# A third of the du*B products of the third stage, moved from GpSimd to ScalarE and TensorE, in a four-block sequence kernel on Trainium2

## The chip, the cores and the metric

The kernel runs on one core of one Trainium2 chip. The metric is the device time of one execution in microseconds (us). Engines are named as in the profile: PE is TensorE (PEld its weight loads), DVE VectorE, ACT ScalarE, POOL GpSimd, and SP the engine whose queue issues most DMAs. Lines are those of the kernel before; in the changed kernel they stand one further down from L623 on.

## What is computed

The input is x of 2 x 1024 x 256. Four blocks follow each other, each adding its output to x after a layer norm: attention with 16 heads of 128 and a causal mask with a linear bias; a feed-forward block with ternary weights; a selective state-space block; and a feed-forward block that keeps two of four hidden values. The change is in the third. Cut to what matters, with 512 channels d (DI) and 16 states n (DN):

```
delta = softplus(dt_low @ dt_proj.T + bias)      # b, l, d
A = -exp(A_log)                                  # d, n
deltaA = exp(delta * A)                          # l, b, d, n
dBu = delta * Bm * x_conv                        # l, b, d, n;  Bm is b, l, n
h = deltaA * h + dBu                             # one step per token l
y = sum over n of h * C  + x_conv * D            # C is b, l, n
out = (y * silu(z)) @ out_proj.T
```

## The kernel before

**Chunks and stages.** The tokens are cut into four chunks of 512 (U), k = 0 to 3: first and second half of sequence 0, then of sequence 1. Attention of chunk k is built together with everything else of chunk k-1 (`rest(k-1)`: ternary feed-forward, state space, kept-two feed-forward). So there are five stages: attention of chunk 0 beside the weight quantization; three stages with attention(k) beside rest(k-1); and rest(3) alone. The **third stage** is attention(2) beside rest(1). There `short` is true: attention(2) is a first half, so its rows of scores are 128 to 512 wide. `tail_end` is true for rest(3) only.

**What orders the work.** Each generator yields a cost after every step (2.2 for a step of the state loop), and the build loop at the end of the kernel runs `rest` ahead until its share of `cost(k)` has reached the share of attention steps done. This fixes the order in which the program is written. A scheduler then sets the order of each engine's queue; on the chip each queue is served in that order. Buffers come from pools: a tile with `bufs` n waits until the tile n earlier of the same tag has been read. PSUM has eight banks of 128 x 512: tag "s" 2 (scores), "mm" 3 (transposes, projections, attention outputs), "y" 1, "r" 2 (everything of `rest`).

**The state loop** (`state_space`, L505 on) goes over 64 products, four groups c of 128 channels times 16 states n. Channels lie on partitions, tokens along the row. For product i the functions are:

- `ask_b`, `ask_c` (L668): SP fetches row n of B and of C from a DRAM copy `bcd`, broadcast to 128 partitions (bs and cs, 256 KB each). bs has 5 buffers and is asked for five products ahead.
- `enter` (L713): POOL multiplies db = du * bs. du = delta * x_conv is made in `steps(c)` (L550 to L554).
- `decay` (L727): ACT computes da = exp(a_neg * dl) into an "r" bank.
- `scan` (L732): DVE runs the recurrence hs = da * h + db along the row. Its start comes from the chunk before (carry).
- `weigh` (L746): POOL multiplies hc = hs * cs, with 5 buffers.
- `total` (L678): PE adds hc into the "y" bank, turned by four 128 x 128 transposes; after n = 15 `gate` copies the sum (L761), turns it back (L764, an "r" bank) and multiplies by sz (L768).

At step i the program has total(i-5), ask_b(i+5), enter(i+1), decay(i), scan(i-1), weigh(i-3), ask_c(i+1).

Before the loop PE computes dt (L534) and bcp (L627), the 32 rows of B and C; ACT copies them (bc, L632), SP writes them to `bcd` (L634), and the broadcasts read them from there.

**The last stage** (`tail_end`) makes no db on POOL. du is turned by PE (`turned`, dup L561) and copied by ACT (duT L565), so that tokens lie on partitions; B as columns (bT, L640, copied as bTs L645) is then one scalar per partition. For n % 5 == 2 ACT scales the four 128 x 128 blocks of duT by it (bu, L697) and PE turns them back into a bank (db, L701); for the others PE multiplies by a diagonal (db, L707). da then lies in SBUF.

Attention's part of a stage, per head: scores s (L357), mask and maximum on DVE (L361, L366), exponential on ACT (L370), transposes pt and copies pT (L288, L291), z (L299, copied as zs L304), projections pq, pk (L330), pv (L337), and o (L313), added to x by DVE (L319). For a first-half chunk kT and v are also stored for the next chunk (kd L345, vd L347, both on SP).

Of the kernel before, what the change touches and what calls it, by code (L numbers as in the profile page):

```python
# [26 lines left out]
DI, DN, DR, DC = 512, 16, 128, 4  # L27
# [14 lines left out]
def kernel(  # L42
# [32 lines left out]
    ps_s, ps_mm, ps_z = bank("s", 2), bank("mm", 3), bank("mm", 3)  # L75
    ps_y, ps_r = bank("y", 1), bank("r", 2)
# [26 lines left out]
    def fill_in():  # L103

        if held:
            with tc.issue_after(ended["by"].ins):
                held.pop(0)()
# [397 lines left out]
    def state_space(k):  # L505
        b, u = CH[k]
        first, last, tail_end = u == 0, u == NU - 1, k == len(CH) - 1
# [3 lines left out]
        with ExitStack() as mctx:  # L511
# [45 lines left out]
            def turned(c, du):  # L557

                tp = ps_r(f"dup_{k}_{c}")
                for t in range(UT):  # L560
                    nc.tensor.transpose(  # L561
                        tp[:, t * P : (t + 1) * P], du[:, t * P : (t + 1) * P], ident
                    )
                duT = row_of("duT", f"duT_{k}_{c}", 2)
                nc.scalar.copy(duT, tp)  # L565
                return duT


            with ExitStack() as ictx:
                mi = ictx.enter_context(tc.tile_pool(name="mi", bufs=1, side="right"))  # L570
                in_sb = mi.tile([P, KC, 2 * DI], F32, name=f"in_sb_{k}")
                nc.sync.dma_start(out=in_sb, in_=inT.rearrange("(c p) m -> p c m", p=P))
                xp_sb = mi.tile([P, NDC, NX], F32, name=f"xp_sb_{k}")
                nc.sync.dma_start(out=xp_sb, in_=xpT.rearrange("(c p) m -> p c m", p=P))
                nc.sync.dma_start(out=dt_sb, in_=dtT)
                nc.sync.dma_start(out=out_sb, in_=outT.rearrange("(c p) m -> p c m", p=P))
                xT, put = plain(mi, f"m{k}")
                layernorm_T(k, f"m{k}", put, ps_r)
                yield 3

                def in_proj(e):
                    pp = (spare(k) if e % 2 else ps_r)(f"in_{k}_{e}")
                    for c in range(KC):
                        nc.tensor.matmul(  # L584
                            pp, lhsT=in_sb[:, c, e * P : (e + 1) * P], rhs=xT[:, c, :],
                            start=(c == 0), stop=(c == KC - 1),
                        )
                    return pp

                for e in range(NDC):  # L590
                    xp = mi.tile([P, DC - 1 + U], F32, tag="xp", name=f"xp_{k}_{e}", bufs=2)
                    if first:
                        nc.gpsimd.memset(xp[:, : DC - 1], 0.0)
                    else:
                        nc.gpsimd.tensor_copy(xp[:, : DC - 1], tail[:, e, :])
                    nc.scalar.copy(xp[:, DC - 1 :], in_proj(e))
                    if not last:
                        nc.gpsimd.tensor_copy(tail[:, e, :], xp[:, U:])
                    acc = work(f"cv_{k}_{e}")
                    nc.vector.tensor_scalar(acc, xp[:, 0:U], cw(e, 0), None, ALU.mult)  # L600
                    for i in range(1, DC):
                        nc.vector.scalar_tensor_tensor(
                            acc, xp[:, i : i + U], cw(e, i), acc, op0=ALU.mult, op1=ALU.add
                        )
                    silus = [nc.scalar.activation(xs[:, e, :], acc, AF.Silu)]
                    yield 3
                for e in range(NDC):
                    silus.append(nc.scalar.activation(sz[:, e, :], in_proj(NDC + e), AF.Silu))
                    yield 2

                with tc.issue_after(silus[0].ins), tc.issue_after(silus[-1].ins):
                    marks.append(nc.scalar.preload_act_table_set("natural_log_exp_and_others"))
                dl_ps = ps_r(f"dtl_{k}")
                for c in range(NDC):
                    nc.tensor.matmul(
                        dl_ps, lhsT=xp_sb[:, c, :DR], rhs=xs[:, c, :],
                        start=(c == 0), stop=(c == NDC - 1),
                    )
                nc.any.tensor_copy(dtl, dl_ps)
                parts, turns = {0: steps(0)}, {}  # L620
                if tail_end:
                    fill_in()
                    turns[0] = turned(0, parts[0][1])  # L623
                yield 3
                bc_ps = ps_da(f"bcp_{k}")
                for c in range(NDC):
                    nc.tensor.matmul(  # L627
                        bc_ps[: 2 * DN, :], lhsT=xp_sb[:, c, DR:], rhs=xs[:, c, :],
                        start=(c == 0), stop=(c == NDC - 1),
                    )  # L630
                bc = mi.tile([2 * DN, U], F32, name=f"bc_{k}", padded_shape=[P, U])
                nc.any.tensor_copy(bc, bc_ps[: 2 * DN, :])  # L632

                nc.sync.dma_start(out=bcd.rearrange("a n t -> (a n) t"), in_=bc)  # L634
                if tail_end:

                    bT_ps = ps_da(f"bT_{k}")[:, : UT * DN].rearrange("p (t n) -> p t n", t=UT)
                    for t in range(UT):
                        for c in range(NDC):
                            nc.tensor.matmul(  # L640
                                bT_ps[:, t, :], lhsT=xs[:, c, t * P : (t + 1) * P],
                                rhs=xp_sb[:, c, DR : DR + DN], start=(c == 0), stop=(c == NDC - 1),
                            )
                    bT = mc.tile([P, UT, DN], F32, name=f"bTs_{k}")
                    nc.vector.tensor_copy(bT, bT_ps)  # L645
                yield 4
# [23 lines left out]
                    )  # L670
                return ask

            ask_b, ask_c = row(brow, 0, "bs", 5), row(crow, 1, "cs", 6 if tail_end else 4)

            def add(c, h, start, stop):

# [6 lines left out]

            by_tensor = lambda i: tail_end
            by_scalar = lambda n: n % 5 == 2

            def enter(i):
                c, n = prods[i]  # L690
                dl, du = parts[c]
                if tail_end and by_scalar(n):

                    db[i] = ps_mm(f"db_{k}_{c}_{n}")
                    bu = part("bu", f"bu_{k}_{c}_{n}", 2)
                    for t in range(UT):
                        nc.scalar.activation(  # L697
                            bu[:, t * P : (t + 1) * P], turns[c][:, t * P : (t + 1) * P], AF.Copy,
                            scale=bT[:, t, n : n + 1],
                        )  # L700
                        nc.tensor.transpose(  # L701
                            db[i][:, t * P : (t + 1) * P], bu[:, t * P : (t + 1) * P], ident
                        )
                elif by_tensor(i):
                    db[i] = ps_mm(f"db_{k}_{c}_{n}")
                    for t in range(UT):
                        nc.tensor.matmul(  # L707
                            db[i][:, t * P : (t + 1) * P], lhsT=turns[c][:, t * P : (t + 1) * P],
                            rhs=diag[:, n, t, :], start=True, stop=True,
                        )  # L710
                else:
                    db[i] = part("db", f"db_{k}_{c}_{n}", 4)
                    nc.gpsimd.tensor_tensor(db[i], du, brow.pop(i), ALU.mult)  # L713
# [9 lines left out]
            def decay(i):  # L723
                c, n = prods[i]
                name = f"da_{k}_{c}_{n}"
                da[i] = part("da", name, 4) if by_tensor(i) else ps_da(name)
                nc.scalar.activation(da[i], parts[c][0], AF.Exp, scale=a_neg[:, c, n : n + 1])  # L727

            def scan(i):
# [45 lines left out]
            for i in range(-5, len(prods) + DRAIN(k)):  # L775
                for lag, f in stages:
                    if 0 <= i - lag < len(prods):
                        f(i - lag)
                if i >= 0:
                    yield 2.2  # L780
                if 0 <= i < len(prods) and i // DN + 1 < NDC:
                    c = i // DN + 1
                    if i % DN == (DN // 4 if tail_end else DN // 2):
                        parts[c] = steps(c)
                        yield 3
                    if tail_end and i % DN == DN - 5:
                        turns[c] = turned(c, parts[c][1])
            for t in range(UT):
                op = (spare(k) if t % 2 else ps_r)(f"mo_{k}_{t}")
# [229 lines left out]
```

## Time and profile before

| | us |
|---|---|
| time, median of 3 runs | 1869.58 (1869.01 to 1869.77) |
| the profiled execution | 1872.9 |
| its span | 1870.9, TensorE clock 0.981 on the mean |
| L746 POOL hc, x256 | 363.9 busy, 1438 ns each |
| L713 POOL db, x192 (three stages) | 258.2 busy, 1352 ns each |
| L727 ACT da, x256 | 177.7 busy, 697 ns each |
| bs from bcd, x192, 256 KB each | 4.4 from issue to landing |
| cs from bcd, x256, 256 KB each | 3.8 from issue to landing |

The span runs from the first to the last recorded instruction; the profiled execution's own time is 2.0 us longer. Busy time is the sum of an engine's instructions in a stretch. The PE clock is the share of full speed that was granted. "Idle before" is the time in which an engine stood still ahead of a group of instructions, with the instruction or transfer that ended it.

### The profile page before, as it was taken

The page shows a single profiled execution, that of the slowest core. Times are in us where ns is not written, and L with a number is a line of the kernel's source. Part 1 is how long each engine was busy: PE and PEld are TensorE (multiplying, and loading weights), DVE is VectorE, ACT ScalarE, POOL GpSimd, SP SyncE. Part 2 cuts the span into 40 slices and gives each one's busy share as a digit, 9 for nine tenths or more (in the row PEclk, how much of TensorE's full clock was granted, in tenths as well). Part 3 has the DMA queues.
Part 4 walks back from the last instruction along what each step waited for, and adds up shares of the span by engine and source line. Part 5 has one row for each costly group of instructions (what it writes and reads, how often), then busy time and mean ns, then how long its engine had stood idle before and what let it go on. Part 6 is the DMA issues. An engine that isn't in the chain of part 4 may idle for free. (4 is left out here: it accounts for less than half of the span.)

```text
span 1870.9 us, 24286 instructions
## 1 busy us (share of the span) xinstructions
PE 1731.3 (93%) x7984; PEld 1156.0 (62%) x7984; DVE 1212.3 (65%) x2347; ACT 959.4 (51%) x1780; POOL 845.5 (45%) x685
## 2 busy tenths in 40 slices
PE   7999999999989999997878999999999999888999
PEld 4666666455656566755556566645665655566895
DVE  5766455677786473468886465567779546446975
ACT  3445474656563562554555446465556345335742
POOL 3324031578892000429996002247889200045970
PEclk9999999999999999999999999999999999888999
DMA  6443512466662311337876324246676320112541
GB/s 188 130 141 127 195 46 86 143 201 204 208 205 83 107 51 60 119 114 231 251 245 196 121 65 133 86 132 198 204 219 203 91 93 32 70 49 73 185 128 62
DMA packets 178285, 255.99 MB, mean 137 GB/s; under 512 B 16224, under 2 KB 90976, under 8 KB 177136
## 3 DMA queue, kind: packets, MB, share of 16 engines
q1 hardware_dynamic: 177008, 241.87, 41.3%
q0 software_dynamic: 1152, 12.58, 1.8%
q8 instruction: 63, 1.03, 0.2%
q14 instruction: 62, 0.51, 0.1%
HBM read 232.04 MB, written 22.35 MB: 136 GB/s over the span
## 5 line engine op out<-in xcount | busy, mean ns | idle before, releaser
L746 POOL TENSOR_TENSOR hc<-hs,cs 128x512 f32<-128x512 f32 x256 | 363.9, 1438 | 16.1 <-PE y L678 9.3
L357 PE MATMUL s<-kT,qT 128*128 128x512 f32 (+3 forms) x768 | 304.7, 498 | 17.1 <-DVE ss L361 15.3
L370 ACT ACTIVATE ss<-ss,nm 128x128 f32<-128x128 f32 (+7 forms) x256 | 198.4, 775 | 178.0 <-DVE nm L366 168.6
L713 POOL TENSOR_TENSOR db<-du,bs 128x512 f32<-128x512 f32 x192 | 258.2, 1352 | 51.8 <-DVE hs L732 43.0
L361 DVE SCALAR_TENSOR_TENSOR ss<-s,lower 128x512 f32<-128x512 f32 (+3 forms) x384 | 204.2, 548 | 112.1 <-PE s L357 110.7
L299 PE MATMUL z<-pT,v 128*128 128x512 f32 (+3 forms) x768 | 266.1, 494 | 10.9 <-ACT pT L291 10.1
L366 DVE CUSTOM_DVE_ANT_0 ss<-ss,alibi 128x128 f32<-128x128 f32 (+7 forms) x256 | 240.6, 942 | 3.4
L727 ACT ACTIVATE da<-dl,a_neg 128x512 f32<-128x512 f32 x256 | 177.7, 697 | 118.1 <-DVE hs L732 94.3
L299 PEld LDWEIGHTS z<-pT,v 128*128 128x128 f32 x768 | 143.4, 191 | 146.2 <-issue 94.1
L291 ACT COPY pT<-pt 128x512 f32<-128x512 f32 (+3 forms) x313 | 142.9, 476 | 174.0 <-PE pt L288 172.3
L288 PE MATMUL pt<-ident,ss 128*128 128x128 f32 x1152 | 181.0, 279 | 38.6 <-DVE x L319 22.9
L288 PEld LDWEIGHTS pt<-ident,ss 128*128 128x128 f32 x1152 | 140.5, 143 | 103.1 <-DVE x L319 38.0
L732 DVE TENSOR_TENSOR_SCAN hs<-da,db 128x512 f32<-128x512 f32 x128 | 154.0, 1211 | 56.6 <-POOL db L713 27.4
L357 PEld LDWEIGHTS s<-kT,qT 128*128 128x128 f32 x768 | 129.0, 195 | 81.0 <-issue 43.9
L732 DVE TENSOR_TENSOR_SCAN hs<-da,carry,db 128x512 f32<-128x512 f32 x128 | 159.0, 1268 | 25.2 <-POOL hc L746 14.4
L319 DVE SCALAR_TENSOR_TENSOR x<-o,rr,x 128x256 f32<-128x256 f32 x256 | 108.9, 475 | 80.7 <-PE o L313 80.6
L678 PE MATMUL y<-ident,hc 128*128 128x128 f32 x1024 | 144.3, 278 | 9.6 <-POOL hc L746 9.6
L337 PEld LDWEIGHTS pv<-wv,xT_a 128*128 128x128 f32 x1024 | 126.1, 194 | 41.4 <-issue 25.4
L448 POOL DMA_DIRECT2D guT<-guT_d x4 | 2.7, 674 | 302.2 <-DVE nm L366 111.0
L337 PE MATMUL pv<-wv,xT_a 128*128 128x128 f32 x1024 | 127.3, 277 | 9.9 <-DVE carry L741 6.5
L678 PEld LDWEIGHTS y<-ident,hc 128*128 128x128 f32 x1024 | 120.7, 145 | 15.3 <-POOL hc L746 12.8
L313 PE MATMUL o<-wo,zs 128*128 128x256 f32 x512 | 123.4, 381 | 4.5 <-ACT kT L333 3.3
(199 smaller groups left out, 2617.6 us busy)
## 6 DMA issues: line engine op xcount, KB each, us to landing
cs<-bcd SPq DMA_DIRECT2D x256, 256.0 KB, 3.8
bs<-bcd SPq DMA_DIRECT2D x192, 256.0 KB, 4.4
alibi<-alibi_d SPq DMA_DIRECT2D x32, 512.0 KB, 4.5
wq<-in_wqT_dram SPq DMA_DIRECT2D x64, 128.0 KB, 3.5
wk<-in_wkT_dram SPq DMA_DIRECT2D x64, 128.0 KB, 3.2
wv<-in_wvT_dram SPq DMA_DIRECT2D x64, 128.0 KB, 2.8
wo<-in_woT_dram SPq DMA_DIRECT2D x64, 128.0 KB, 2.8
alibi<-alibi_d SPq DMA_DIRECT2D x32, 256.0 KB, 3.6
```

The lines of the kernel that those rows point to most:

```text
L288: nc.tensor.transpose(tp[:, i, :], s[:, (kb0 + i) * P : (kb0 + i + 1) * P], ident)
L299: nc.tensor.matmul(zp[:, q0:], lhsT=st["v_all"][:, kb, :], rhs=st["pts"][kb // 4][:, kb % 4, q0:], start=(kb == 0), stop=(kb == last),)
L337: nc.tensor.matmul(vp[:, t, :], lhsT=xT[:, c, t * P : (t + 1) * P], rhs=st["v"][:, c, :], start=(c == 0), stop=(c == KC - 1),)
L357: nc.tensor.matmul(sp[:, :n], lhsT=st["qT"][:, j * P : (j + 1) * P], rhs=st["kT"][:, k0 : k0 + n], start=True, stop=True,)
L361: nc.vector.scalar_tensor_tensor(s[:, k0 : k0 + n], sp[:, :n], CLIP, lower[:, S - W + k0 : S - W + k0 + n], op0=ALU.min, op1=ALU.max,)
L366: pace["tile"] = nc.vector.tensor_tensor_reduce(out=s[:, :W], in0=s[:, :W], in1=st["alibi"][:, :W], scale=1.0, scalar=3.0e38, op0=ALU.add, ...
L370: nc.scalar.activation(s[:, :W], s[:, :W], AF.Exp, bias=nm, scale=-1.0, accum_out=st["rs"][:, j : j + 1])
L678: nc.tensor.matmul(yTs[c][:, t * P : (t + 1) * P], lhsT=h[:, t * P : (t + 1) * P], rhs=ident, is_transpose=True, start=start and t == 0, s ...
L713: nc.gpsimd.tensor_tensor(db[i], du, brow.pop(i), ALU.mult)
L727: nc.scalar.activation(da[i], parts[c][0], AF.Exp, scale=a_neg[:, c, n : n + 1])
L732: nc.vector.tensor_tensor_scan(out=hs[i], data0=da.pop(i), data1=db.pop(i), initial=0.0 if first else carry[:, n, c : c + 1], op0=ALU.mult ...
L746: nc.gpsimd.tensor_tensor(hc[i], hs.pop(i), crow.pop(i), ALU.mult)
```

## The change

For k = 1 (`short`) the products with n % 3 == 1, that is n = 1, 4, 7, 10 and 13 of each c, 20 of 64, are made as in the last stage's n % 5 == 2: du is turned and copied (duT, one buffer), ACT scales four blocks of it by B's columns (bu, one buffer), and PE turns them back, into an "r" bank. Their da goes to SBUF (two buffers); the other 44 da stay in "r" banks. No row of B is fetched for these 20, and bs has four buffers instead of five. bT is computed in this stage too, and `turned` is called right after `steps(0)`, ahead of bcp, and later at n = 11 for the next c. The last stage is as before.

```diff
-                duT = row_of("duT", f"duT_{k}_{c}", 2)
+                duT = row_of("duT", f"duT_{k}_{c}", 2 if tail_end else 1)
...
                 if tail_end:
                     fill_in()
+                if tail_end or short:
                     turns[0] = turned(0, parts[0][1])
...
                 nc.sync.dma_start(out=bcd.rearrange("a n t -> (a n) t"), in_=bc)
-                if tail_end:
+                if tail_end or short:
 
                     bT_ps = ps_da(f"bT_{k}")[:, : UT * DN].rearrange("p (t n) -> p t n", t=UT)
...
-            ask_b, ask_c = row(brow, 0, "bs", 5), row(crow, 1, "cs", 6 if tail_end else 4)
+            ask_b, ask_c = row(brow, 0, "bs", 4 if short else 5), row(crow, 1, "cs", 6 if tail_end else 4)
...
-            by_tensor = lambda i: tail_end
-            by_scalar = lambda n: n % 5 == 2
+            by_scalar = lambda n: (tail_end and n % 5 == 2) or (short and n % 3 == 1)
+            by_tensor = lambda i: tail_end or by_scalar(prods[i][1])
...
-                if tail_end and by_scalar(n):
-
-                    db[i] = ps_mm(f"db_{k}_{c}_{n}")
-                    bu = part("bu", f"bu_{k}_{c}_{n}", 2)
+                if by_scalar(n):
+
+                    db[i] = (ps_mm if tail_end else ps_r)(f"db_{k}_{c}_{n}")
+                    bu = part("bu", f"bu_{k}_{c}_{n}", 2 if tail_end else 1)
                     for t in range(UT):
                         nc.scalar.activation(
                             bu[:, t * P : (t + 1) * P], turns[c][:, t * P : (t + 1) * P], AF.Copy,
...
-                da[i] = part("da", name, 4) if by_tensor(i) else ps_da(name)
+                da[i] = part("da", name, 4 if tail_end else 2) if by_tensor(i) else ps_da(name)
...
-                    if tail_end and i % DN == DN - 5:
+                    if (tail_end or short) and i % DN == DN - 5:
                         turns[c] = turned(c, parts[c][1])
```

## The prediction

> **What bounds the kernel now.** I read the page's first part, then tables of windows until the stage of the change stood alone, then groups and waits inside it. The whole span:
>
> ```profile
> PE 1731.3 (93%) x7984; PEld 1156.0 (62%) x7984; DVE 1212.3 (65%) x2347; ACT 959.4 (51%) x1780; POOL 845.5 (45%) x685
> ```
>
> By the average TensorE bounds the kernel and GpSimd has room. The state loop of the third stage (834 to 1015 us) is another matter. Columns: window, length, busy PE, PEld, DVE, ACT, POOL (instructions), PE clock, DMA share, GB/s.
>
> ```profile
> 834.00:860.00 26.00, 22.21 (x114) 15.40 (x113) 20.49 (x28) 12.97 (x27) 23.52 (x19) 1.00 0.74 240
> 860.00:880.00 20.00, 14.24 (x69) 9.68 (x67) 17.70 (x24) 11.34 (x25) 19.92 (x16) 0.91 0.83 250
> ...
> 900.00:920.00 20.00, 16.08 (x81) 11.26 (x80) 15.93 (x22) 10.16 (x20) 19.79 (x16) 0.84 0.81 260
> ...
> 960.00:980.00 20.00, 12.61 (x60) 8.17 (x60) 17.00 (x22) 8.60 (x18) 19.80 (x16) 1.00 0.66 219
> 980.00:1000.00 20.00, 17.93 (x98) 12.66 (x98) 16.59 (x28) 13.38 (x27) 20.00 (x16) 1.00 0.81 245
> ...
> 1015.00:1030.00 15.00, 15.00 (x84) 12.12 (x83) 8.02 (x24) 5.74 (x15) 0.29 (x1) 1.00 0.28 90
> ```
>
> See POOL at 19.8 to 20.0 of 20 from 860 to 1000, PE at 12.6 to 17.9, and PE full as soon as POOL is done. Over 834:1015 the sums are POOL 174.5, DVE 147.4, PE 145.9, ACT 95.7 of 181 us: PE idles 35.1. The groups of that window (count | busy us, mean ns | idle before, releaser):
>
> ```profile
> L713 POOL TENSOR_TENSOR db<-du,bs 128x512 f32<-128x512 f32 x64 | 85.9, 1348 | 5.1 <-DMA bs<-bcd 4.6 <-POOL du L554 0.4
> L746 POOL TENSOR_TENSOR hc<-hs,cs 128x512 f32<-128x512 f32 x64 | 85.5, 1341 | 2.8 <-DMA cs<-bcd 2.8
> L732 DVE TENSOR_TENSOR_SCAN hs<-da,carry,db 128x512 f32<-128x512 f32 x64 | 80.4, 1271 | 17.8 <-POOL hc L746 14.4 <-POOL db L713 1.9 <-ACT da L727 1.4
> L727 ACT ACTIVATE da<-dl,a_neg 128x512 f32<-128x512 f32 x62 | 42.8, 691 | 34.5 <-DVE hs L732 34.4
> ```
>
> POOL does 128 multiplications back to back; the scans wait for its buffers. PE's largest waits, 820:1020 (total us, times, longest):
>
> ```profile
> PE y L678 <- POOL hc L746: 9.1, 8, 3.1
> PE pt L288 <- DVE x L319: 8.0, 6, 2.4
> ```
>
> Only the first is POOL's directly. Since PE is 94 to 98% busy in 1000:1200, ending the loop early pays only as far as PE loses idle time inside it.
>
> **The change, part by part.** For 20 of the 64 products (n = 1, 4, 7, 10, 13; four c) the POOL multiplication goes. What replaces it runs in the last stage already (1705:1812):
>
> ```profile
> L697 ACT ACTIVATE bu<-duT,bTs 128x128 f32<-128x128 f32 x48 | 15.7, 387 | 0.0
> L701 PE MATMUL db<-ident,bu 128*128 128x128 f32 x48 | 8.2, 284 | 1.0 <-DVE hs L732 1.0
> L561 PE MATMUL dup<-ident,du 128*128 128x128 f32 x12 | 1.8, 272 | 0.0
> ```
>
> *POOL*: 20 x 1.348 = 27.0 us go: 147.5 left.
> *ACT*: 80 x 0.327 (15.7/48) = 26.2, four duT copies at 0.58 = 2.3, 20 exponentials into SBUF at 0.718 instead of 0.691 = 0.5: 95.7 becomes 125 of 181. Hidden, as ACT has 85 idle; without that cover 29.
> *PE*: 80 transposes at 0.150 (36.3/242, the y transposes of this loop) to 0.171 (8.2/48) = 12.0 to 13.7; dup 16 x 0.15 = 2.4; bT 3.7 (once, as at 1701.2). Sum 18 to 20: 145.9 becomes 165.
> *Clock*: the granted mean is 0.94 here, and dips follow PE's idle moments (910:915 has 2.58 busy of 5, then 915:920 a clock of 0.50). Spread evenly over busy PE the missing 0.06 would be 145.9 x 0.06 = 9 us; as the dips lie at idle moments I count 0 to 7. So 158 to 165; I take 162.
> *DVE*: the bTs copy, 0.2; the scans cost the same from PSUM (1.266 in the last stage).
> *DMA*: 20 rows of 256 KB fewer. Four bs buffers for 44 rows span six products, five for 64 spanned five: the 4.6 us of waits for bs do not grow; bounds -4.6 and 0, I take 0.
>
> The Trainium skill ("TensorE: Matmul & The Clock Gate", Part 4: PE-mode transpose) speaks against this: about 275 ns for one transpose, and transposes do not keep the clock up. By it the 80 would cost 22 us and PE's sum be 9 higher. The rows record 272 to 293 ns each too, but overlapping: busy time per transpose is 0.15 to 0.17. And 1726:1746, with 175 matmuls of that size, half of them transposes, ran at clock 1.00.
>
> *The start, where something is moved.* In the changed queues PE turns du (dup) before it computes bcp, so bcp moves from right behind dt (825.2) to behind du. Three score rows on DVE are now ahead of sr, so du ends at about 833.5 (831.8 before); four transposes, 834.3; bcp 3.6, 837.9; bc 0.57, 838.5. Before, bc's end (829.4) to the first db (834.5) took 5.1: first db 843.6. On SP, two loads (an alibi row, wq) now stand ahead of the bcd write, and wk and the store of kd between it and the first bs; kd waits for kT, which waits for pk, which PE does behind bT: bT to 841.6, pk and kT to 843.2, then 3.3 from request to db as before: 846.5. The loop's start is 9 to 12 us late (best case 0, if SP's order costs nothing and bcp slips forward). PE does attention meanwhile (it was full in 820:834), so this is POOL's loss, not PE's: bank 27 - 9 to 12 = 15 to 18 for POOL's path.
>
> *New waits.* The loop's exponentials used two PSUM banks alternately, each waiting for the scan two back. Now a turned product holds one of the banks from its transposes to its scan, so 44 exponentials wait for the scan just ahead, and the next scan for them: up to 0.69 + handover. A handover is 0.04 (a scan ended at 882.31, the exponential began at 882.35); I bound it by 0.1 on each side, so 0 to 0.9 per exponential, 0 to 40 in sum. Queued on ACT behind them are score exponentials and pT copies that PE's z needs. The static order puts DVE's other work (147.4 - 80.4 = 67 us, 1.05 per product) mostly into those gaps, so I take them as covered. bu has one buffer, so ACT also waits for PE to turn the last one, and PE does z, pq, pk, pv and o in one piece of about 10 us per head; a scan behind it waits, but the order places DVE's x updates there.
>
> **Sum.** Next limits for the stage: POOL 147.5 + 9 to 12 late = 157 to 160; DVE 147; PE 162 at a share it can reach. It reached 0.92 in the fourth stage (202.2 of 220 in 1230:1450, POOL 0.83, DVE 0.77) and 0.90 in the last (90.2 of 100). 162/0.92 = 176 against 181: 5 us. Break-even: PE may idle 16 to 23 instead of 35. The profiled execution took 1872.9 (span 1870.9 and 2.0 around it), 3.3 over the median of 1869.58; I subtract the gain from either: 1867.9 by profile, **1864.6** by median.
>
> **Rivals.**
> *A (forecast, 0.42)*: PE becomes the bound at 0.90 to 0.94: 0 to 9 us, centre 5: 1864.6, own range 1861 to 1869. For: PE full after the loop, POOL no longer late. A difference under 0.2% (3.7 us), about what a measurement can tell, takes 0.08 of it.
> *B (0.16)*: PE packs to 0.95 at full clock, 158/0.95 = 166; POOL's path gives the same 15 us: 1855 (up to 1852). For: 1015:1030 and 1100:1200 run at 0.98 to 1.00. Against: DVE at 147/166 = 0.89 and in order.
> *C (0.12)*: the removed wait is replaced: PE waits for x, pT, zs (8.0, 3.7, 3.4 above y's 9.1) stay, share about 0.895: 181 again, 1870. This is also how it looks if the change relieves POOL and nothing else. 0.08 within, 0.02 to each side.
> *D, slower (0.30)*: the bank wait. Place: ACT's exponential behind DVE's scan. The stage is 9 late + DVE 147 + 44 x uncovered part; it decides from (181 - 156)/44 = 0.57 us each. At 0.8: 191, +10: 1880. Upper end with 12 and 0.9: 199, +18: 1887. For: ACT's 34.4 us of waits for scans show how tightly the two are coupled with two banks free.
>
> Faster 0.32 + 0.02 + 0.16 = 0.50; same 0.08 + 0.08 = 0.16; slower 0.02 + 0.02 + 0.30 = 0.34 (0.02 of A falls there). Range 1853 to 1885: it leaves out a quarter of B and a third of D, under 2 in 10.
>
> **What would show it.** Right: L713 in the stage x44, about 59 us; POOL near 0.84; PE 0.91 or more; clock about 1.00; first db 843 to 847; y's wait for hc below 5 us. D: scans waiting for exponentials 15 us or more (1.4 now). B: the last hc before 1002. Wrong altogether: PE busy over 170, or a first db later than 850.

## The result, and the profile after

The changed kernel takes 1877.17 us in the median of 7 runs (1874.44 to 1880.48), the kernel before 1870.37 in 7 runs. The ratio is 1.0031 with a 95% interval of 1.0018 to 1.0043: 5.8 us slower, 3.4 to 8.0 (the medians lie 6.8 apart). The forecast was 1864.6, the range 1853 to 1885; the time lies in the range, and the sign of the forecast was wrong. Single executions far above the others of their kernel, one of e14 at 2575 us and one of e15 at 6248, are left out of the ratios below, and e14's profile is of that one. The profiled execution of the changed kernel took 1880.48 with a span of 1878.7, 7.8 over the span before.

The first part of the page of the changed kernel:

```profile
PE 1744.5 (93%) x8112; PEld 1167.0 (62%) x8112; DVE 1208.0 (64%) x2355; ACT 981.5 (52%) x1857; POOL 818.1 (44%) x665
```

PE has 13 us more, ACT 22 more, POOL 27 less. The same windows as in the prediction, of the changed kernel (columns as there):

```profile
834.00:860.00 26.00, 20.16 (x114) 14.97 (x112) 13.69 (x21) 12.56 (x30) 12.32 (x10) 0.87 0.56 176
860.00:880.00 20.00, 16.81 (x83) 11.57 (x84) 16.71 (x24) 12.82 (x29) 17.95 (x15) 0.91 0.71 219
...
900.00:920.00 20.00, 18.72 (x107) 13.84 (x108) 14.06 (x28) 13.66 (x33) 13.03 (x11) 1.00 0.82 270
...
940.00:960.00 20.00, 15.79 (x96) 10.99 (x95) 20.00 (x33) 14.79 (x36) 19.42 (x16) 1.00 0.81 265
960.00:980.00 20.00, 17.44 (x98) 12.70 (x97) 17.92 (x25) 14.97 (x37) 17.86 (x15) 1.00 0.62 192
980.00:1000.00 20.00, 18.20 (x108) 13.28 (x107) 16.61 (x28) 13.38 (x32) 17.39 (x15) 1.00 0.83 253
...
1015.00:1030.00 15.00, 14.86 (x77) 10.90 (x78) 6.87 (x19) 6.38 (x17) 2.54 (x2) 1.00 0.24 80
```

From 860 to 1000 no engine is full throughout any more: POOL lies at 13.0 to 19.4 of 20, PE at 15.8 to 18.7, and DVE fills one window, 940:960. So POOL was relieved, and PE did not take up the room.

For a measure of the stage that no change of order blurs I take the time from the first matmul of dtl (L615, ahead of the start) to the first of mo (L791, behind the loop). One window each, kernel before, then changed kernel:

```profile
819.90:1025.00 205.10, 169.96 (x837) 117.45 (x837) 159.05 (x242) 109.41 (x226) 177.38 (x136) 0.95 0.71 221
```

```profile
819.30:1029.10 209.80, 182.72 (x966) 128.74 (x965) 155.78 (x250) 131.59 (x303) 150.59 (x116) 0.96 0.61 191
```

The stage is 4.7 us longer. PE's busy time rises by 12.8 and its idle time falls by 8.0, from 35.1 to 27.1: that is the whole account. (The other 3 of the span's 7.8 us lie elsewhere, and this execution is the longest of its seven; I give them no cause.)

The groups of the changed kernel in 834:1015:

```profile
L747 POOL TENSOR_TENSOR hc<-hs,cs 128x512 f32<-128x512 f32 x63 | 82.3, 1315 | 14.7 <-issue 2.5 <-PE s L357 2.2 <-DVE x L319 2.0
L733 DVE TENSOR_TENSOR_SCAN hs<-da,carry,db 128x512 f32<-128x512 f32 x63 | 78.6, 1266 | 7.2 <-ACT da L728 4.3 <-POOL db L714 2.9
L714 POOL TENSOR_TENSOR db<-du,bs 128x512 f32<-128x512 f32 x44 | 60.1, 1369 | 15.4 <-DMA bs<-bcd 15.4
L698 ACT ACTIVATE bu<-duT,bTs 128x128 f32<-128x128 f32 x80 | 27.0, 388 | 4.2 <-PE db L702 4.1
L702 PE MATMUL db<-ident,bu 128*128 128x128 f32 x80 | 14.7, 296 | 9.0 <-ACT pT L291 4.7 <-DVE hs L733 3.4 <-DVE xs L769 0.6
```

The waits of DVE, then of PE, 820:1029 (total us, times, longest):

```profile
DVE ss L361 <- PE s L357: 16.4, 8, 7.0
DVE x L319 <- PE o L313: 11.5, 7, 4.5
DVE bTs L646 <- PE bT L641: 9.2, 1, 9.2
```

```profile
PE y L679 <- POOL hc L747: 7.1, 7, 1.8
PE db L702 <- ACT pT L291: 4.7, 1, 4.7
PE dup L561 <- POOL du L554: 3.5, 2, 2.2
PE db L702 <- DVE hs L733: 3.4, 5, 1.5
PE dt L534 <- DVE hs L733: 1.8, 2, 1.3
```

The first two in the kernel before:

```profile
DVE ss L361 <- PE s L357: 16.7, 5, 8.7
DVE x L319 <- PE o L313: 3.0, 2, 1.5
```

There DVE waited another 14.4 us for POOL's hc. So its wait for s is as it was, and the scans no longer wait for POOL's buffers. In place of that, DVE, which serves its queue in order, stands 8.5 us longer in front of PE's o, with the next scans queued behind, and once, at the start, 9.2 in front of bT.

On PE the waits for DVE's x (8.0 before, in the prediction's lines) are gone, and y's wait for hc is 7.1 instead of 9.1. Half of what is left of PE's idle time, 13.5 of 27.1 us, lies directly ahead of the added instructions: 9.0 ahead of the transposes (L702 above) and 4.5 ahead of dup (3.5 for POOL's du, 1.0 for a scan).

The start, POOL and then SP of the changed kernel (start, duration, instruction, idle before it):

```profile
847.68 3.70 POOL L714 TENSOR_TENSOR db<-du,bs 128x512 f32<-128x512 f32 x3 [15.39 <-DMA bs<-bcd]
```

```profile
837.19 0.32 SPq L635 DMA_DIRECT2D bcd<-bc  x1
841.21 0.38 SPq L262 DMA_DIRECT2D wk<-in_wkT_dram  x1
841.84 0.34 SPq L345 DMA_DIRECT2D kd<-kT  x1
842.28 0.86 SPq L669 DMA_DIRECT2D bs<-bcd  x2
```

The first db is at 847.7, 13.1 us later than before. The loop itself, from the first db to the last hc, is 171.7 us long, against 180.8: 9.1 shorter. Read alone, these two numbers say that the late start ate the gain. It was the first theory, and e1 and e7 refuted it.

### The profile page after: what moved, and what is told of

Read it like the earlier page. It is cut to its first block, busy times and chain, and to the rows that moved or that the text cites. A ratio compares the mean times of both kernels' runs of the same rounds, so it can differ in the third digit from the quotient of the medians.

```text
span 1878.7 us, 24573 instructions
## 1 busy us (share of the span) xinstructions
PE 1744.5 (93%) x8112; PEld 1167.0 (62%) x8112; DVE 1208.0 (64%) x2355; ACT 981.5 (52%) x1857; POOL 818.1 (44%) x665
## 5 line engine op out<-in xcount | busy, mean ns | idle before, releaser
L357 PE MATMUL s<-kT,qT 128*128 128x512 f32 (+3 forms) x768 | 306.6, 499 | 17.6 <-DVE ss L361 16.6
L714 POOL TENSOR_TENSOR db<-du,bs 128x512 f32<-128x512 f32 x172 | 230.0, 1343 | 62.7 <-DVE hs L733 43.9
L366 DVE CUSTOM_DVE_ANT_0 ss<-ss,alibi 128x128 f32<-128x128 f32 (+7 forms) x256 | 233.7, 915 | 3.3
L288 PE MATMUL pt<-ident,ss 128*128 128x128 f32 x1152 | 179.3, 277 | 24.3 <-DVE x L319 14.9
L288 PEld LDWEIGHTS pt<-ident,ss 128*128 128x128 f32 x1152 | 139.6, 142 | 87.2 <-DVE x L319 27.1
L733 DVE TENSOR_TENSOR_SCAN hs<-da,carry,db 128x512 f32<-128x512 f32 x128 | 158.7, 1267 | 14.8 <-ACT da L728 4.3
L679 PEld LDWEIGHTS y<-ident,hc 128*128 128x128 f32 x1024 | 120.2, 144 | 15.4 <-POOL hc L747 10.9
```

Source lines behind the costliest of these rows:

```text
L288: nc.tensor.transpose(tp[:, i, :], s[:, (kb0 + i) * P : (kb0 + i + 1) * P], ident)
L357: nc.tensor.matmul(sp[:, :n], lhsT=st["qT"][:, j * P : (j + 1) * P], rhs=st["kT"][:, k0 : k0 + n], start=True, stop=True,)
L366: pace["tile"] = nc.vector.tensor_tensor_reduce(out=s[:, :W], in0=s[:, :W], in1=st["alibi"][:, :W], scale=1.0, scalar=3.0e38, op0=ALU.add, ...
L679: nc.tensor.matmul(yTs[c][:, t * P : (t + 1) * P], lhsT=h[:, t * P : (t + 1) * P], rhs=ident, is_transpose=True, start=start and t == 0, s ...
L733: nc.vector.tensor_tensor_scan(out=hs[i], data0=da.pop(i), data1=db.pop(i), initial=0.0 if first else carry[:, n, c : c + 1], op0=ALU.mult ...
```

## The experiments

Ratios are to the kernel before on the same chip; 0.001 is 1.87 us. "Stage" is the window from dtl to mo in one profile; a profiled execution can lie off the median of its kernel (e13's took 1864.2, its median is 1869.1; e2's 1886.9, its median 1891.1), so the ratio decides where the two differ.

| run | ratio (95% interval) | us against before | stage, us |
|---|---|---|---|
| before | 1 | 0 | 205.1 |
| the change | 1.0031 (1.0018 to 1.0043) | +5.8 | 209.8 |
| e1_bc_first | 1.0038 (1.0021 to 1.0056) | +7.1 | 209.2 |
| e7_bc_first_own_xp | 1.0032 (1.0020 to 1.0044) | +6.0 | 209.4 |
| e8_no_late_start | 1.0010 (0.9998 to 1.0021) | +1.9 | 206.2 |
| e4_n5 | 1.0072 (1.0045 to 1.0099) | +13.5 | 211.9 |
| e3_db_in_mm | 1.0157 (1.0129 to 1.0185) | +29 | 231.0 |
| e2_start_only | 1.0103 (1.0077 to 1.0129) | +19 | 223.0 |
| e6_added_only | 1.0260 (1.0243 to 1.0277) | +49 | 250.4 |
| e5_relief_only | 0.9924 (0.9910 to 0.9938) | -14.2 | 190.4 |
| e9_relief_pe_held | 0.9956 (0.9940 to 0.9972) | -8.2 | 199.5 |
| e10_relief_act | 0.9948 (0.9934 to 0.9962) | -9.7 | 194.3 |
| e11_relief_pe_free | 1.0042 (1.0029 to 1.0056) | +7.9 | 212.9 |
| e12_relief_late | 0.9976 (0.9966 to 0.9986) | -4.5 | 201.1 |
| e13_relief_pe_mm | 0.9989 (0.9965 to 1.0013) | -2.1 | 200.9 |
| e14_relief_dup_bT | 0.9965 (0.9948 to 0.9983) | -6.5 | not read |
| e15_dve_8 | 1.0005 (0.9990 to 1.0021) | +0.9 | 205.9 |

### The late start

**e1_bc_first**: turning du moves behind the write of bcd.

```diff
-                if tail_end or short:
+                if tail_end:
                     turns[0] = turned(0, parts[0][1])
...
                 nc.sync.dma_start(out=bcd.rearrange("a n t -> (a n) t"), in_=bc)
+                if short:
+                    turns[0] = turned(0, parts[0][1])
```

> The changed kernel with one call moved: du is turned behind the write of bcd, so that bcp, bc and the first rows of B come as early as in the kernel before; the loop is that of the changed kernel. Theory L (late start): in the changed kernel's profile the first db is 13.1 us later than before (847.7 against 834.5) and the loop itself 9.0 us shorter (171.7 from the first db to the last hc, against 180.8). With the start back at 834 to 838 the kernel should be 5 to 9 us faster than before: 1861 to 1865 where before is 1870. Rival W (waits inside the loop: bank, ACT queue, PE on both sides of the scan): the start is hidden by attention, and this run stays near the changed kernel, 1874 to 1878.

Measured: 1.0038, as slow as the changed kernel, as rival W has it. The first db came 8.2 us after du instead of 15.4 (2.7 before), and the loop took 179.3. What the start gained the loop gave back.

**e7_bc_first_own_xp**: the same, and B's columns of the projection in a tile of their own, so that the loop's buffers do not wait for bT.

```diff
+                if short:
+                    xpb = mc.tile([P, NDC, DN], F32, name=f"xpb_{k}")
+                    nc.sync.dma_start(
+                        out=xpb, in_=xpT[:, DR : DR + DN].rearrange("(c p) m -> p c m", p=P)
+                    )
...
-                                rhs=xp_sb[:, c, DR : DR + DN], start=(c == 0), stop=(c == NDC - 1),
+                                rhs=xpb[:, c, :] if short else xp_sb[:, c, DR : DR + DN], start=(c == 0), stop=(c == NDC - 1),
```

> e1_bc_first again, but B's columns of the projection lie in a tile of their own, loaded beside the rest, so that the buffers of the loop need not wait for bT (in e1_bc_first the first row of B was requested at 834.6, 5 us after the write of bcd had landed, when bT had ended). The first db should be 2 to 3 us after du, as before. Theory P: the loop grows by what the start gains: 1875 to 1879, as e1_bc_first. Theory L (late start): 4 to 5 faster than e1_bc_first, 1871 to 1875.

Measured: 1.0032. The start is fully restored (POOL of this run):

```profile
834.86 3.72 POOL L721 TENSOR_TENSOR db<-du,bs 128x512 f32<-128x512 f32 x3 [2.88 <-DMA bs<-bcd]
```

The loop now takes 184.4 us, longer than that of the kernel before with 20 multiplications more. So the short loop of the changed kernel was an effect of its late start: PE had done more of attention's work ahead of it, 60 matmuls from dtl to the first db, against 12 in e7 and 23 in the kernel before. Neither number alone is a gain or a loss; only the stage is.

**e2_start_only**: the changed start, no product moved.

```diff
-            by_scalar = lambda n: (tail_end and n % 5 == 2) or (short and n % 3 == 1)
+            by_scalar = lambda n: tail_end and n % 5 == 2
...
-                    if (tail_end or short) and i % DN == DN - 5:
+                    if tail_end and i % DN == DN - 5:
```

> The other half: dup, duT and bT of the changed kernel at their places ahead of the loop, and its order of the start, but no product is moved (all 64 db by GpSimd, five bs buffers). duT and bTs of this stage are computed and not used. Theory L: the loop is as long as before, 180.8, and begins 10 to 13 us late: 1878 to 1883 where before is 1870. Rival W: the start is covered by attention's work on PE, so only the 6 us of added PE work show at most: 1870 to 1876.

Measured: 19 us slower, 8 beyond theory L's 1878 to 1883 (loop 185.7, 4.9 longer than before). With POOL as the limit the lateness is paid, and more than the lateness (the first db is 11.8 us later behind du than before); with POOL relieved (e7 against the change) it is not. What a late start costs depends on which engine is the limit.

**e8_no_late_start**: moved products only for c = 1 to 3, bT inside the loop.

```diff
-            by_scalar = lambda n: (tail_end and n % 5 == 2) or (short and n % 3 == 1)
+            by_scalar = lambda n, c=1: (tail_end and n % 5 == 2) or (short and c > 0 and n % 3 == 1)
...
+                    if short and i == 4:
+                        bT = columns(xpb)
```

> No late start at all: the first group of channels keeps its 16 multiplications on GpSimd, bT is computed inside the loop at its fifth step, and only 15 products (n = 1, 4, 7, 10, 13 of the last three groups) are moved. Theory L: GpSimd saves 15 x 1.35 = 20 us and begins on time: 1858 to 1864. Theory P: PE's added work is 3.7 + 1.8 + 60 x 0.16 = 15 us, paid nearly in full against a relief of 12 to 15: 1868 to 1874.

Measured: 1.0010, not to be told from before: theory P's number.

**e4_n5** and **e3_db_in_mm**, both on top of e1: twelve products, and the turned products in attention's banks.

```diff
-            by_scalar = lambda n: (tail_end and n % 5 == 2) or (short and n % 3 == 1)
+            by_scalar = lambda n: (tail_end and n % 5 == 2) or (short and n % 5 == 2)
```

```diff
-                    db[i] = (ps_mm if tail_end else ps_r)(f"db_{k}_{c}_{n}")
+                    db[i] = ps_mm(f"db_{k}_{c}_{n}")
```

> As e1_bc_first with 12 products moved (n = 2, 7, 12) instead of 20. Theory L: the loop's gain goes with the number as long as GpSimd bounds the loop: 12/20 of 9 us, so 2 to 5 us slower than e1_bc_first and 3 to 6 faster than before. Rival W: fewer waits, so faster than e1_bc_first.

> As e1_bc_first, but the turned products go to a bank of attention's tag mm (3 banks) instead of r, so the 44 exponentials alternate between two r banks as before. Theory L: no effect beyond 2 us to either side of e1_bc_first. Rival W: the bank wait costs up to 0.9 us for each of 44, so 4 us or more faster than e1_bc_first, unless attention's transposes now wait for banks.

Measured: 1.0072 and 1.0157. Theory L had e4 2 to 5 us slower than e1, but faster than before; it is 6 slower than e1 and 13 slower than before. Less relief at the same price of dup and bT points that way, but not by 6 us (the stage of its profile is 2.7 longer than e1's); why stays open. In e3 attention pays: DVE's zs waits 14.8 us for PE's z, which hardly happened before, and the scans wait 17.6 us for PE's db.

### The relief and the additions, each alone

**e5_relief_only**: the kernel before without the 20 multiplications.

```diff
+            skipped = lambda n: short and n % 3 == 1
...
+                elif skipped(n):
+                    db[i] = db[i - 1]
```

> The kernel before with the 20 multiplications of GpSimd (n = 1, 4, 7, 10, 13 of the third stage) and their rows of B left out and nothing in their place: the scan reads the db of the product ahead of it, so these 20 products of the states are not computed. Start and PE work are those of the kernel before. Theory P (the work added to PE is paid nearly in full, since PE and DVE wait for each other in their fixed orders once GpSimd no longer limits): the relief alone is worth most of its 27 us, 12 to 20: 1851 to 1858 where before is 1870. Rival C (GpSimd was busy but not the limit; the order of PE and DVE is): 0 to 5 faster, 1865 to 1870.

Measured: 0.9924, 14.2 us faster. Theory C falls: GpSimd was the limit, and its relief is worth half of its 27 us. (20 fetched rows of B go with the multiplications; POOL had waited 4.6 us for such rows before, and waits 4.9 here.) The stage:

```profile
819.70:1010.10 190.40, 169.57 (x838) 117.54 (x837) 155.50 (x242) 109.97 (x226) 151.94 (x116) 0.94 0.67 211
```

PE's busy time is that of before, its idle time 20.8. Its share is 169.6/190.4 = 0.89, with this relief and nothing added: the highest seen in this stage.

**e9_relief_pe_held**, **e10_relief_act**, **e12_relief_late**: each adds one part of the change to e5.

```diff
                 elif skipped(n):
-                    db[i] = db[i - 1]
+                    db[i] = ps_r(f"db_{k}_{c}_{n}")
+                    for t in range(UT):
+                        nc.tensor.transpose(
+                            db[i][:, t * P : (t + 1) * P], du[:, t * P : (t + 1) * P], ident
+                        )
```

```diff
                     db[i] = db[i - 1]
+                    bu = part("bu", f"bu_{k}_{c}_{n}", 1)
+                    for t in range(UT):
+                        nc.scalar.activation(
+                            bu[:, t * P : (t + 1) * P], du[:, t * P : (t + 1) * P], AF.Copy,
+                            scale=a_neg[:, c, n : n + 1],
+                        )
```

e12 is e2_start_only with e5's edit. Two differences come along: e9 puts the 20 products' da in SBUF, as the change does, and e9 and e10 (and e11 below) have four bs buffers instead of e5's five. POOL's waits for bs hardly differ (4.2 and 5.6 us in e9 and e10, 4.9 in e5).

> e5_relief_only plus PE's share alone: for each of the 20 products PE turns four blocks of du itself (no scaling by B, so these products are wrong in value) into an r bank, and the scan reads that bank; their exponentials go to SBUF. No ACT work, no dup, no bT, start as before. Theory P (PE's added time is what is paid): 80 x 0.16 = 13 us on top of e5_relief_only's 1857: 1867 to 1872. Rival B (what is paid is the waiting: the bank held until the scan): the same sum if waits replace work, but then e11 with the same work and no held bank is 4 or more faster than this one.

> e5_relief_only plus ACT's share alone: 80 scaled 128x128 blocks (of du, by a column of a_neg) into a buffer that nothing reads. Theory P: ACT has room, 0 to 2 us over e5_relief_only: 1857 to 1860. Rival A (ACT's queue delays the exponentials and pT copies): 4 to 8 over it, 1861 to 1865.

> e5_relief_only with the start of the changed kernel (dup, bcp behind it, bT; 13 us late). Theory P: POOL has slack once relieved, so the late start shows only as PE's work, 0.7 + 3.7 us, and little waiting: 1861 to 1866. Theory L (late start): 10 or more over e5_relief_only, 1867 to 1872.

Measured over e5, from the ratios: PE's transposes +6.0 us (0.0032, give or take 0.0021), ACT's blocks +4.5 (0.0024, 0.0020), start with dup and bT +9.7 (0.0052, 0.0017). The sum is 20.2; the whole change lies 0.0107, or 20.0 us, over e5. The agreement is closer than the intervals warrant, but no large part is missing. The stages of e9, e10 and e12:

```profile
819.30:1018.80 199.50, 177.29 (x918) 125.57 (x917) 150.06 (x240) 112.17 (x229) 151.57 (x116) 0.95 0.64 201
```

```profile
818.50:1012.80 194.30, 166.82 (x839) 114.02 (x838) 159.80 (x249) 129.58 (x300) 150.23 (x116) 0.97 0.66 206
```

```profile
820.60:1021.70 201.10, 174.60 (x875) 120.65 (x874) 156.37 (x242) 111.71 (x229) 151.35 (x116) 0.94 0.67 199
```

In e9 PE is 7.7 us busier than in e5 and the stage 9.1 longer: added PE work is paid about in full, although PE idled 20.8. Theory P had the price too high, 13 us for the 80 transposes and 1867 to 1872; the median is 1865.3. The scans of e9 wait 13.3 us for exponentials, against 4.3 in the changed kernel, which fits rival B; e13 below is the test of it. In e10 PE does no more work and idles 6.7 longer: ACT's blocks, on an engine that is still a third free, delay what is queued behind them. So theory A has something, and theory P's 0 to 2 us for ACT was too low. e12, at 1867.2, lies above P's 1861 to 1866 and at the lower end of L's 1867 to 1872.

**e14_relief_dup_bT** parts e12's work from its lateness: dup and bT at e7's places, first db on time.

```diff
-            by_scalar = lambda n: (tail_end and n % 5 == 2) or (short and n % 3 == 1)
+            by_scalar = lambda n: tail_end and n % 5 == 2
+            skipped = lambda n: short and n % 3 == 1
...
+                elif skipped(n):
+                    db[i] = db[i - 1]
```

> e5_relief_only plus dup of the first group and bT, at the places of e7_bc_first_own_xp: 4.4 us of PE work ahead of the loop, and the first db on time. Beside e12_relief_late (9.7 us over e5_relief_only, with the same PE work and a first db 13 us late). Theory P: the PE work is what is paid in e12, so 4 to 7 over e5_relief_only, and no more than 4 under e12. Theory L: the lateness is paid, so 0 to 3 over it.

Measured: 0.9965, +7.7 over e5 (0.0041, give or take 0.0022), 2 under e12 (0.0010, give or take 0.0020). This is just above theory P's 4 to 7, and outside theory L's 0 to 3. So with POOL relieved most of e12's price goes with PE's 4.4 us of work ahead of the loop, not with the lateness; whether 4.4 us of work really cost 7.7 stays open, as the interval covers both. That e14 starts on time is taken from e7; its own start was not read.

**e11_relief_pe_free** and **e13_relief_pe_mm**: the same PE work as e9, with no bank held until the scan.

```diff
-                    db[i] = ps_r(f"db_{k}_{c}_{n}")
+                    db[i] = db[i - 1]
+                    unread = ps_r(f"db_{k}_{c}_{n}")
```

e13 has `unread = ps_mm(...)`, and leaves all 64 exponentials in r banks.

> As e9_relief_pe_held, but the scan reads the db of the product ahead of it, so that the bank with the turned blocks is free as soon as PE is done. Theory P: as e9, 1867 to 1872, within 2 us of it. Rival B: 4 or more faster than e9.

> e11 mended: e5_relief_only (all 64 exponentials in r banks, so that every scan reads its da from PSUM as before) plus 80 transposes of blocks of du into banks of the tag mm that nothing reads. PE's work alone, with no bank of the loop held and no scan that waits for PE. The products are as wrong as in e5_relief_only. Theory P (PE's time is what is paid): 8 to 13 us over e5_relief_only's 1857, near e9_relief_pe_held (1865) or above. Rival B (the held bank and the scan's wait for PE are paid): 0 to 3 over e5_relief_only. And if e11's extra 15 us came from scans with both operands in SBUF (its 64 scans took 1477 ns on the mean against 1266), this run has scans of 1.27 us and is far from e11's 1880.

Measured: e11 16 us slower than e9 (neither theory's number), e13 +12.2 over e5 (0.0065, give or take 0.0028), in theory P's 8 to 13 and outside rival B's 0 to 3. The stage of e13:

```profile
818.50:1019.40 200.90, 178.00 (x919) 124.70 (x918) 156.96 (x246) 108.35 (x223) 150.33 (x116) 0.95 0.64 200
```

PE is 8.4 us busier than in e5 and idles 22.9; in e9 it was 7.7 and 22.2. So e13 is not faster than e9: taking the held bank away gained nothing. The test is not clean, as e13's transposes go to attention's banks, where e3 lost 22 us against e1; that they cost nothing there is not shown. (The scans wait 6.4 us for exponentials in e13, half of e9's 13.3.) e11 is no test of a held bank: its 20 products have both operands of the scan in SBUF (last section).

**e6_added_only**: the changed kernel, with GpSimd's 64 multiplications kept.

```diff
-                    db[i] = (ps_mm if tail_end else ps_r)(f"db_{k}_{c}_{n}")
+                    bank_of = (ps_mm if tail_end else ps_r)(f"db_{k}_{c}_{n}")
+                    db[i] = bank_of
+                    if short:
+                        db[i] = part("db", f"dbp_{k}_{c}_{n}", 4)
+                        nc.gpsimd.tensor_tensor(db[i], du, brow.pop(i), ALU.mult)
```

> The changed kernel with its additions, and GpSimd's 64 multiplications kept: dup, bT, 80 scaled blocks and 80 transposes are made, into r banks that nothing reads, while the scans take GpSimd's db. Beside e2_start_only (1891, the start without the products) it tells what the 80 blocks and transposes cost while GpSimd is the limit. Theory P: GpSimd at its limit hides most, 1890 to 1896. Rival C: PE's and ACT's added work is paid here too, 1899 to 1905.

Measured: 1.0260, beyond both. It has e11's trouble as well, so it tells nothing of P against C.

**e15_dve_8**: another engine takes the work.

```diff
-                    nc.gpsimd.tensor_tensor(db[i], du, brow.pop(i), ALU.mult)
+                    eng = nc.vector if short and n % 8 == 4 else nc.gpsimd
+                    eng.tensor_tensor(db[i], du, brow.pop(i), ALU.mult)
```

> The kernel before with 8 of the 64 multiplications of the third stage (n = 4 and 12) made by DVE in place of GpSimd; nothing is added to PE, ACT or the start. GpSimd is relieved by 8 x 1.35 = 10.8 us, which by e5_relief_only is worth 14.2 x 8/20 = 5.7; DVE, 147 of 181 busy and ahead of PE in a ring, gets 8 x 0.7 to 1.7 = 6 to 14. Theory P (any engine of the ring PE, DVE, ACT pays in full what is added to it): 0 to 8 slower than before. Rival: DVE's 34 idle us take it, 3 to 6 faster.

Measured: 1.0005, no difference: theory P's range, not the rival's. The eight multiplications took DVE 10.1 us (0.66 to 1.78 each); GpSimd's db fell by 8.1, from 85.9 to 77.8, instead of 10.8, as the other 56 became slower (1392 ns against 1348). No version that keeps the computation beats the kernel before.

## Why the prediction was wrong, point by point

**What bounds the stage: right.** POOL bounded the loop; e5 shows what its relief is worth, 14.2 us. My ceiling for POOL's path, 15 to 18, was near that, though for another reason: PE's idle time in e5 ends at 20.8, not at the cost of a late start. (POOL at "19.8 to 20.0 of 20 from 860 to 1000" was misread: 940:960 has 19.3.)

**The added work: right, with luck in the sum.** L714 has 44 instructions and 60.1 us (59 foretold), bu 27.0 (26.2), bT 3.7. The 80 transposes took 14.7, 0.18 each (12.0 to 13.7), dup 3.0 (2.4). These rows of PE sum to 21.4, above the 18 to 20 foretold, but PE's busy time in the stage rose by 12.8 only. I had 12 to 19, and took 16, by counting on a higher clock, which did not come. In e9 the row of the 80 transposes is 12.8 us and PE's busy time rises by 7.7. The rows of a stage overlap on PE (before, all of them sum to 192.9 us where the stage has 170.0 busy), so a sum of rows overstates what they add.

**The clock: wrong.** It stayed at 0.96 (0.95 before), where about 1.00 was to be seen. At the loop's start, 834:860, where PE idled 5.8 of 26 us, it was 0.87; but 940:960, with 4.2 idle of 20, ran at 1.00, so that the idle time sets it is not shown.

**The start: right in size, wrong in worth.** 9 to 12 us late was foretold, 13.1 came (847.7, just past the 843 to 847 of the signs); the first rows of B took 5.4 us from request to db, not 3.3. I counted it as POOL's loss. e7 shows that the changed kernel loses nothing by it, as POOL has slack there.

**The failed step** is this one: "PE 162 at a share it can reach. It reached 0.92 in the fourth stage". The share was 0.87 (182.7/209.8; in the prediction's own window, 834:1015, 155.3 of 181, 0.86, where 0.91 or more was to be seen). PE's idle time was 27.1 where the break-even stood at "16 to 23 instead of 35", and at 22.3 with the 12.8 us by which its work really rose. The share was taken from another stage, with rows of scores two to three times as long and so more PE work per product (202.2 us in that window against 145.9 in this loop); that this is why it was no measure here is argued, not shown. e5 has 0.89 with nothing added. At 0.89 the changed kernel's 182.7 us of PE work take 205, exactly the stage before: at the best share that was seen here the change is worth nothing. ACT's blocks, foretold as hidden ("ACT has 85 idle"), take another 4.5 us (give or take 3.7).

**The rivals.** D's price was near (1880; 1877 measured), but its mechanism is not borne out: scans waited 4.3 us for exponentials, where I had asked for 15, and e13 without a held bank is no faster than e9. Scarce banks do show on the other side: 6.8 of PE's 27.1 idle us, ahead of db, dt and dup, which go to r banks, end with DVE's scans (3.4, 1.8 and 1.0) or xs (0.6), which read such banks; the kernel before has none of these. No run takes them away alone. C had the outline, "the removed wait is replaced", at too low a price: I priced it at no change, with 0.12. Of the waits that it expected to stay, that for x is gone and that for zs is 0.4, and those ahead of the added instructions came in their place. y's wait for hc, 7.1, also missed its sign (below 5).

**What is shown and what is argued.** Shown: the relief's worth, the cost of each addition on top of it, that the late start is not paid in the changed kernel. Made unlikely, not excluded: that the held bank is the main cause. Argued from the queues, with the waits beside it: why PE's idle time cannot be used. PE, DVE, ACT and POOL serve fixed orders that cross in both directions (PE's o and s before DVE's next scan, the scan before POOL's hc, hc before PE's y), so a microsecond added to one delays the next in turn. Open: why twelve products (e4) cost more than twenty (e1), and what the r banks cost by themselves.

## What to carry to other kernels

Before work is moved off a full engine, leave it out without a replacement and measure: this gives the ceiling (here 14 us of the 27 saved), and the additions must cost less than that. Idle time of an engine that takes turns with others in fixed orders is not room: here added PE work was paid about in full at a busy share of 0.89 (e9 on e5), and added ACT work in part, 4.5 of 19.6 us, at 0.58 (e10 on e5). And a loop that became shorter says nothing while work can move across its start; measure between two instructions that the change does not touch.

## What the runs showed of the hardware

A scan with one operand in PSUM took 1.25 to 1.28 us in e6; with both in SBUF it took up to 2.33. The first row has da in PSUM, the second in SBUF; db is in SBUF in both (count, then min/median/max in ns):

```profile
L737 DVE TENSOR_TENSOR_SCAN hs<-da,carry,db x44: 1251/1269/1283, 851.0 to 1054.8; 128x512 f32<-128x512 f32 x44
L737 DVE TENSOR_TENSOR_SCAN hs<-da,carry,dbp x20: 1252/2137/2326, 852.3 to 1051.1; 128x512 f32<-128x512 f32 x20
```

GpSimd loses too: its hc in e6 took 1465 ns on the mean, against 1341 in the kernel before. The Trainium skill ("SBUF — State Buffer", SBUF: two separate sides) says that a DVE instruction with two SBUF inputs and a GpSimd instruction that reads SBUF hold one pair of ports in turn; the minimum of 1252 and the median of 2137 agree with a wait for one GpSimd instruction. It is a reason to keep da in PSUM where db is in SBUF, and it is why e6 and e11 are no clean tests.
